# Sparse attention over listed keys: half steps taken in pairs, and a new order of the steps' parts on the PE

## The chip, the cores and the metric

The kernel runs on one core of a Trainium2 chip. The time is the device time of one execution, in microseconds. Before the change the median of three runs is 2332.32 us (2330.68 to 2333.52). The engines are named as in the profile: PE multiplies matrices (PEld is its weight loads, which run beside the multiplications), ACT is ScalarE, DVE is VectorE, POOL is GpSimd, which issues the gathers here, and SP issues the plain transfers.

## The reference

One layer of graph attention with 8 heads over 4096 nodes, in which a node attends only to its neighbours, and then a mixture of 8 experts of which each node takes two. All is f32. The change concerns the attention:

```python
q = jnp.einsum('nd,hdk->hnk', node_matrix, Wqs)        # 8 heads of 64
k = jnp.einsum('nd,hdk->hnk', node_matrix, Wks)
v = jnp.einsum('nd,hdk->hnk', node_matrix, Wvs)
scores = jnp.einsum('hqk,hmk->hqm', q, k) * kd ** (-0.5)
scores = scores + IDENTITY_BIAS * eye - MASK_VAL * (1.0 - adj)
att = jax.nn.softmax(scores, axis=-1)
return jnp.einsum('hqm,hmk,hko->qo', att, v, Wo)
```

The adjacency is sparse, and a node's own entry always counts as set.

## The kernel before

The kernel has three stages. The first normalizes x, computes q, k and v, writes a row of k and v per node to memory, and makes a list of keys for each tile of 128 queries: the nodes that any query of the tile has as a neighbour, 128 of them to a "key tile". The second is the attention over those lists, with the end of each tile of queries (division by the sums, product with Wo, routing to experts) mixed into its steps. The third is the experts. Only the second changes.

A list has three parts: keys that only the first 64 queries of the tile need, keys that both halves need, and keys that only the last 64 need. A step takes one key tile `(i, c)`. For keys of both halves it works on 128 queries (a full step), for the others on 64 (a half step, `half_of` gives the half). `c = -1` is the step of the tile's own 128 nodes, the diagonal, a full one. The list lengths give 32 diagonal, 134 full and 229 half steps, 395 in all.

For each step POOL gathers the 128 rows of k and v (4 KB each) and, unless they were packed before, those of the mask. PE then transposes k, multiplies it with q, ACT takes the exponential, DVE multiplies by the mask, PE multiplies with the values into the tile's output `po`, and DVE adds the weights to the sums `acc`. q lies in a tile of twice its size: for each pair of heads p, `q_in[:, p, 0]` holds the even head's 64 rows with zeros below, `q_in[:, p, 1]` the odd head's with zeros above. (Two memory clears on POOL write the zeros once.)

```python
        def turn(n):
            kT[n] = work.tile([P, NP, P], F32, tag="kT", bufs=3, name=f"kT_{n}")
            pk = ps_k.tile([P, 2, TB], F32, tag="k", name=f"pk_{n}")
            for p in range(NP):
                for r in range(2):
                    half = slice(r * KD, (r + 1) * KD)
                    nc.tensor.transpose(
                        pk[:, r, ts(p, KD)], kv[n][half, ts(p, P)], ident[half, half]
                    )
            nc.scalar.copy(
                kT[n].rearrange("k p (r j) -> k r p j", r=2),
                pk[:, :, : NP * KD].rearrange("k r (p j) -> k r p j", p=NP),
            )

# ... (queries(i, c): the 128 or 64 columns of the step)
        def scores(n):
            i, c = items[n]
            full = half_of(i, c) is None
            q = queries(i, c)
            k = kT.pop(n)
            if c < 0:
                e = two.tile([P, H, P], F32, tag="acc", name=f"acc_{i}")
                acc[i] = e
            else:
                e = work.tile([P, H, P], F32, tag="e", name=f"e_{i}_{c}")
                if not full:
                    e = e.rearrange("p h q -> p (h q)")[:, : H * QH]
                    e = e.rearrange("p (h q) -> p h q", h=H)
            es[n] = e
            if full:
                s = [
                    ps_s.tile([P, NP, P], F32, tag="s", name=f"s{r}_{i}_{c}") for r in range(2)
                ]
                for p in range(NP):
                    for r in range(2):
                        rows = slice(r * KD, (r + 1) * KD)
                        nc.tensor.matmul(
                            s[r][:, p, :], k[rows, p, :], q_in[i][rows, p, r, :],
                            start=True, stop=True,
                        )
                for r in range(2):
                    nc.scalar.activation(
                        e.rearrange("p (a r) q -> p r a q", r=2)[:, r], s[r], AF.Exp
                    )
            else:
                s = ps_s.tile([P, NP, 2, QH], F32, tag="s", name=f"s_{i}_{c}")
                for p in range(NP):
                    nc.tensor.matmul(
                        s[:, p], k[:, p, :], q_in[i][:, p, :, q], start=True, stop=True
                    )
                nc.scalar.activation(e, s.rearrange("p a r q -> p (a r) q"), AF.Exp)
        def masked(n):
            i, c = items[n]
            e, m = es[n], mask.pop(n)
            if c < 0:
                nc.vector.tensor_max(m, m, eye_d)
            m = mask_part(m, i, c)
            nc.vector.tensor_mul(e, e, m.unsqueeze(1).to_broadcast(e.shape))
        def values(n):
            i, c = items[n]
            e = es.pop(n)
            if c < 0:
                po[i] = ps_o.tile([P, NP, P], F32, tag="o", name=f"po_{i}")
            v = kv.pop(n)[:, H * KD :]
            q = queries(i, c)
            for h in range(H):
                p, r = divmod(h, 2)
                nc.tensor.matmul(
                    po[i][r * KD : (r + 1) * KD, p, q], v[:, ts(h, KD)], e[:, h, :],
                    start=(c < 0 and p == 0), stop=(c == listed[i] - 1),
                    skip_group_check=True,
                )
            if c >= 0:
                nc.vector.tensor_add(acc[i][:, :, q], acc[i][:, :, q], e)

```

The loop works three steps ahead with the transposes and two with the scores; `fetch` starts the gathers nine steps ahead. `later` issues the parts of finished tiles, of which those after 1, 3 and 5 steps multiply on PE, and the jobs of the routing, one in a step without such a part.

```python
        def later(n):
            busy = False
            for n0, i in left:
                piece(i, n - n0)
                busy = busy or n - n0 in (1, 3, 5)
            if jobs and not busy:
                then = jobs.pop(0)()
                if then:
                    first_of_step.append(then)
        for n in range(3):
            turn(n)
        for n in range(2):
            scores(n)
            masked(n)
        loads = [(e, c) for e in range(E) for c in range(DC)]
        for n, (i, c) in enumerate(items):
            begin()
            if n + AHEAD < len(items):
                fetch(n + AHEAD)
            if c == 2 and i + 1 < NT:
                load_q(i + 1)
            if c == min(7, listed[i] - 1):
                load_x(i)
            if n >= 56 and n % 7 == 0 and loads:
                e, d = loads.pop(0)
                nc.sync.dma_start(out=w1[:, e, d], in_=W1[e, ts(d, P), :])
            if c < 0 and i:
                osb[i - 1] = single.tile([P, NP, P], F32, tag="o", name=f"o_{i - 1}")
                nc.scalar.copy(osb[i - 1], po.pop(i - 1))
            if n + 3 < len(items):
                turn(n + 3)
            if n + 2 < len(items):
                scores(n + 2)
            values(n)
            later(n)
            if n + 2 < len(items):
                masked(n + 2)
            if c == listed[i] - 1:
                left.append((n, i))
        osb[NT - 1] = single.tile([P, NP, P], F32, tag="o", name=f"o_{NT - 1}")
        nc.scalar.copy(osb[NT - 1], po.pop(NT - 1))

```

The pools of PSUM: three buffers for scores (`ps_s`), one for the transposes (`ps_k`, two banks), one for the output `po`, two for the ends of tiles.

## Time and profile before

The profile covers one execution, whose span is 2307.7 us.

| engine | busy us | share of the span |
|---|---|---|
| PE | 2102.1 | 91% |
| PEld | 1389.0 | 60% |
| DVE | 1266.7 | 55% |
| POOL | 1030.9 | 45% |
| ACT | 933.3 | 40% |

The attention loop takes from about 465 to 1692 us of it, the experts from about 1800 us to the end. The groups of instructions that matter here, from the fifth part of the page (all in that loop):

| what | count | busy us | mean ns |
|---|---|---|---|
| PE transposes of k (L917) | 2904 | 177.5 | 239 |
| PE scores of half steps, K = 128 (L964) | 1832 | 276.2 | 295 |
| PE scores of full steps, K = 64 (L952) | 2144 | 160.2 | 283 |
| PE products with the values (L987) | 5808 | 322.4 | 250 |
| ACT copy of the transposed k (L920) | 395 | 232.3 | 588 |
| ACT exponentials of full (L957) and half (L967) steps | 268 and 229 | 146.9 and 137.9 | 597 and 602 |
| DVE product with the mask (L975) | 363 | 322.3 | 888 |
| DVE sum of the weights (L993) | 363 | 320.5 | 883 |

How to read it: an f32 product is recorded as two matmuls and two weight loads. PE's matmuls are pipelined and their ends are modelled, so a busy PE is not PE at its peak; what can be read closely is when an instruction starts. "64*128 64x128" is a stationary operand of 64 rows and 128 columns, and a moving one of 64 rows and 128 columns. Diagonal steps have names of their own in the profile, and are not in all of these counts.

### The profile page before, as it was taken

How to read it: one execution, taken by the hardware profiler on the slowest of the kernel's cores; microseconds unless marked ns; L12 is line 12 of the kernel's file. 1: busy time of each engine (PE TensorE's matmuls, PEld its weight loads, DVE VectorE, ACT ScalarE, POOL GpSimd, SP SyncE). 2: the span in 40 equal slices, each digit the busy share in tenths (PEclk: the TensorE clock that was granted, in tenths of full speed). 3: DMA queues.
4: the chain of work that ended last, by engine and by line, in shares of the span. 5: the costliest groups of instructions: out<-in, count | busy, mean ns of one | idle time of the engine just before them, and what ended most of it. 6: DMA issues, size and time to landing. Idle time of an engine off the chain costs nothing. (4 is left out here: it accounts for less than half of the span.)

```text
span 2307.7 us, 48617 instructions
## 1 busy us (share of the span) xinstructions
PE 2102.1 (91%) x18796; PEld 1389.0 (60%) x18796; DVE 1266.7 (55%) x2297; ACT 933.3 (40%) x1709; POOL 1030.9 (45%) x1080
## 2 busy tenths in 40 slices
PE   7988897899999889999999999998957999999998
PEld 3434443387777777777777777776733444444444
DVE  4686676166666656656656666665652332323332
ACT  2644443355445445445445454544421222222221
POOL 1044434667666566565555655566521121212112
PEclk9998999899999999999899999999978999999999
DMA  7777877667777777778777877767666656665564
GB/s 293 313 264 269 273 261 248 207 192 212 225 242 233 221 235 234 220 219 234 211 234 223 237 220 225 224 197 225 186 237 148 134 137 136 137 138 134 137 132 91
DMA packets 214383, 481.13 MB, mean 208 GB/s; under 512 B 49234, under 2 KB 81234, under 8 KB 210052
## 3 DMA queue, kind: packets, MB, share of 16 engines
q0 software_dynamic: 79232, 242.18, 37.1%
q1 hardware_dynamic: 133764, 233.68, 33.0%
q8 instruction: 153, 2.51, 0.4%
q10 hardware_dynamic: 1152, 2.10, 0.3%
q14 instruction: 82, 0.67, 0.1%
HBM read 400.43 MB, written 77.42 MB: 207 GB/s over the span
## 5 line engine op out<-in xcount | busy, mean ns | idle before, releaser
L228 POOL DMA_INDIRECT kv<-kv_d,key_of x363 | 405.8, 1118 | 384.4 <-PE po L987 220.5
L975 DVE TENSOR_TENSOR e<-e,mask 128x512 f32<-128x512 f32 (+1 forms) x363 | 322.3, 888 | 308.1 <-ACT e L967 144.3
L920 ACT COPY kT<-pk 128x512 f32<-128x512 f32 x395 | 232.3, 588 | 370.6 <-PE pk L917 216.6
L987 PE MATMUL po<-e,kv 128*64 128x64 f32 (+1 forms) x5808 | 322.4, 250 | 18.2 <-issue 17.9
L1387 POOL DMA_INDIRECT out_dram<-y,r x71 | 110.6, 1558 | 473.7 <-ACT y L1386 453.2
L993 DVE TENSOR_TENSOR acc<-acc,e 128x512 f32<-128x512 f32 (+1 forms) x363 | 320.5, 883 | 2.5 <-PE sums L1012 0.9
L228 POOL DMA_INDIRECT mask<-in_adjT_dram,mask_of x234 | 282.3, 1206 | 72.9 <-issue 63.4
L987 PEld LDWEIGHTS po<-e,kv 128*64 128x64 f32 x5808 | 251.9, 139 | 70.1 <-issue 25.8
L964 PE MATMUL s<-q,kT 128*128 128x128 f32 x1832 | 276.2, 295 | 3.1 <-issue 2.7
L1351 PE MATMUL ph<-w,xT 128*128 x568 | 257.9, 597 | 0.7 <-ACT xT L207 0.7
L1380 PE MATMUL py<-w,hT 128*128 x568 | 255.6, 593 | 0.9 <-DVE hT L1365 0.9
L964 PEld LDWEIGHTS s<-q,kT 128*128 128x128 f32 x1832 | 230.8, 197 | 19.4 <-issue 3.5
L917 PE MATMUL pk<-ident,kv 64*128 64x64 f32 x2904 | 177.5, 239 | 49.0 <-ACT kT L920 30.1
L917 PEld LDWEIGHTS pk<-ident,kv 64*128 64x128 f32 x2904 | 123.9, 141 | 120.2 <-issue 72.0
L228 POOL DMA_INDIRECT pm<-in_adjT_dram,mask_of x129 | 126.2, 978 | 149.6 <-DMA packed_h<-pm 80.0
L957 ACT ACTIVATE e<-s 128x512 f32<-128x512 f32 x268 | 146.9, 597 | 72.1 <-PE s L952 30.1
L1385 DVE TENSOR_TENSOR y<-py,bb 128x512 f32<-128x512 f32 x71 | 49.1, 692 | 225.6 <-PE py L1380 225.6
L967 ACT ACTIVATE e<-s 128x512 f32<-128x512 f32 x229 | 137.9, 602 | 79.4 <-PE s L964 43.9
L359 DVE TENSOR_REDUCE flags<-adjT 128x64 f32<-128x4096 f32 x32 | 141.0, 4408 | 52.3 <-DMA adjT<-in_adjT_dram 52.3
L1351 PEld LDWEIGHTS ph<-w,xT 128*128 128x128 f32 x568 | 103.1, 192 | 103.8 <-issue 102.7
L1380 PEld LDWEIGHTS py<-w,hT 128*128 128x128 f32 x568 | 102.5, 190 | 104.0 <-issue 102.8
L952 PE MATMUL s<-q,kT 64*128 64x128 f32 x2144 | 160.2, 283 | 4.6 <-issue 2.6
(598 smaller groups left out, 2614.8 us busy)
## 6 DMA issues: line engine op xcount, KB each, us to landing
adjT<-in_adjT_dram SPq DMA_DIRECT2D x32, 2048.0 KB
bb<-in_L_ffn_b_dram SPq DMA_DIRECT2D x142, 256.0 KB
r<-xs_d SPq DMA_DIRECT2D x71, 258.0 KB
kv_d<-kv SPq DMA_DIRECT2D x32, 512.0 KB
xt<-in_x_dram SPq DMA_DIRECT2D x32, 256.0 KB
qT_d<-qT SPq DMA_DIRECT2D x8, 1024.0 KB
q<-qT_d SPq DMA_DIRECT2D x64, 128.0 KB
xr<-in_x_dram SPq DMA_DIRECT2D x32, 256.0 KB
```

Source lines behind the costliest of these rows:

```text
L228: nc.gpsimd.indirect_dma_start(out=to, out_offset=None, in_=src, in_offset=bass.IndirectOffsetOnAxis(ap=of[:, at[i] + c : at[i] + c + 1], ...
L359: nc.vector.tensor_reduce(flags[g][:, :, j, :], adj_in.pop(i).rearrange("p c (h q) -> p h c q", h=2), axis=AX.X, op=ALU.max,)
L917: nc.tensor.transpose(pk[:, r, ts(p, KD)], kv[n][half, ts(p, P)], ident[half, half])
L920: nc.scalar.copy(kT[n].rearrange("k p (r j) -> k r p j", r=2), pk[:, :, : NP * KD].rearrange("k r (p j) -> k r p j", p=NP),)
L952: nc.tensor.matmul(s[r][:, p, :], k[rows, p, :], q_in[i][rows, p, r, :], start=True, stop=True,)
L957: nc.scalar.activation(e.rearrange("p (a r) q -> p r a q", r=2)[:, r], s[r], AF.Exp)
L964: nc.tensor.matmul(s[:, p], k[:, p, :], q_in[i][:, p, :, q], start=True, stop=True)
L975: nc.vector.tensor_mul(e, e, m.unsqueeze(1).to_broadcast(e.shape))
L987: nc.tensor.matmul(po[i][r * KD : (r + 1) * KD, p, q], v[:, ts(h, KD)], e[:, h, :], start=(c < 0 and p == 0), stop=(c == listed[i] - 1), s ...
L993: nc.vector.tensor_add(acc[i][:, :, q], acc[i][:, :, q], e)
L1351: nc.tensor.matmul(ph, xTs[b][:, c, :], w1[:, bass.ds(es[b], 1), c, :], start=(c == 0), stop=(c == DC - 1),)
L1380: nc.tensor.matmul(py, hTs[b][:, c, :], w2[:, bass.ds(es[b], 1), c, :], start=(c == 0), stop=(c == HC - 1),)
```

## The change

Half steps are worked on by two. A unit is a diagonal, a full key tile, or a pair of half ones (one alone where their number is odd); pairs and full ones alternate evenly over a tile's list. A pair has one exponential per parity of heads, one product with the mask per parity, one copy of the transposed keys, and one place in the loop. All scores are now taken from 64 rows of q and k, even heads in the upper and odd ones in the lower rows, so that q needs no zeros and comes in one transfer. The two parities lie in two banks, and each has its own exponential and its own product with the mask, the second of which is issued a step later. In a step PE is given the transposes of the unit after next, the values of this one, the ends of tiles and the scores of the unit after next. The copy of the output follows the tile's last values at once. Gathers run eleven key tiles ahead. A step with a pair may take a job of the routing beside another piece.

It is for giving PE fewer and larger steps, with fewer changes between kinds of work, and the same work of ACT and DVE in larger operations for pairs.

The diff, cut to its core:

```diff
-    AHEAD = 9
-    items = [(i, c) for i in range(NT) for c in range(-1, listed[i])]
+    KEPT = 11
+
+    units = []
+    for i in range(NT):
+        units.append((i, [-1]))
+        alone = [c for c in range(listed[i]) if half_of(i, c) is not None]
+        pairs = [alone[j : j + 2] for j in range(0, len(alone), 2)]
+        both = [[c] for c in range(listed[i]) if half_of(i, c) is None]
+        few, total = len(pairs), len(pairs) + len(both)
+        for j in range(total):
+            if j * few // total < (j + 1) * few // total:
+                units.append((i, pairs.pop(0)))
+            else:
+                units.append((i, both.pop(0)))
+    keys_of = [(n, j) for n, (i, cs) in enumerate(units) for j in range(len(cs))]
+    first_key = [sum(len(cs) for _, cs in units[:n]) for n in range(len(units))]
+    fetched = []
... (load_q in one transfer; fetch by keys, the masks of a pair in one tile; pools)
         def turn(n):
+            i, cs = units[n]
+            kT[n] = work.tile([P, 2, NP, P], F32, tag="kT", bufs=2, name=f"kT_{n}")
             pk = ps_k.tile([P, 2, TB], F32, tag="k", name=f"pk_{n}")
+            for j in range(len(cs)):
+                for p in range(NP):
+                    for r in range(2):
+                        half = slice(r * KD, (r + 1) * KD)
+                        nc.tensor.transpose(
+                            pk[:, r, ts(j * NP + p, KD)], kv[n, j][half, ts(p, P)],
+                            ident[half, half],
+                        )
+            m = len(cs) * NP
             nc.scalar.copy(
+                kT[n].rearrange("k j p (r c) -> k r (j p) c", r=2)[:, :, :m],
+                pk.rearrange("k r (m c) -> k r m c", c=KD)[:, :, :m],
             )
         def queries(i, c):
             h = half_of(i, c)
             return slice(0, P) if h is None else ts(h, QH)
+        def width(n):
+            i, cs = units[n]
+            return P if half_of(i, cs[0]) is None else len(cs) * QH
+        def heads(e):
+            return e.rearrange("p (a r) q -> p r a q", r=2)
         def scores(n):
+            i, cs = units[n]
+            w = width(n)
             k = kT.pop(n)
+            ss[n] = []
+            for r in range(2):
+                s = ps_s.tile([P, NP * P], F32, tag="s", name=f"s{r}_{n}")
+                ss[n].append(s[:, : NP * w].rearrange("p (a q) -> p a q", a=NP))
+            for j, c in enumerate(cs):
+                m = w // len(cs)
                 for p in range(NP):
                     for r in range(2):
                         rows = slice(r * KD, (r + 1) * KD)
                         nc.tensor.matmul(
+                            ss[n][r][:, p, ts(j, m)], k[rows, j, p, :],
+                            q_in[i][rows, p, queries(i, c)], start=True, stop=True,
                         )
+            if cs[0] < 0:
+                es[n] = acc[i] = two.tile([P, H, P], F32, tag="acc", name=f"acc_{i}")
+                nc.vector.tensor_max(mask[n], mask[n], eye_d)
+            else:
+                e = work.tile([P, H * P], F32, tag="e", name=f"e_{n}")
+                es[n] = e[:, : H * w].rearrange("p (h q) -> p h q", h=H)
+        def masked(n, r):
+            w = width(n)
+            e = heads(es[n])[:, r]
+            nc.scalar.activation(e, ss[n][r], AF.Exp)
+            nc.vector.tensor_mul(
+                e, e, mask[n][:, :w].unsqueeze(1).to_broadcast([P, NP, w])
+            )
+        def values(n):
+            i, cs = units[n]
+            e = es.pop(n)
+            last = n + 1 == len(units) or units[n + 1][0] > i
+            if cs[0] < 0:
+                po[i] = ps_o.tile([P, NP, P], F32, tag="o", name=f"po_{i}")
+            m = width(n) // len(cs)
+            for j, c in enumerate(cs):
+                v = kv.pop((n, j))[:, H * KD :]
+                for h in range(H):
+                    p, r = divmod(h, 2)
+                    nc.tensor.matmul(
+                        po[i][r * KD : (r + 1) * KD, p, queries(i, c)], v[:, ts(h, KD)],
+                        e[:, h, ts(j, m)], start=(c < 0 and p == 0),
+                        stop=(last and j == len(cs) - 1), skip_group_check=True,
                     )
+            if last:
+                osb[i] = single.tile([P, NP, P], F32, tag="o", name=f"o_{i}")
+                nc.scalar.copy(osb[i], po.pop(i))
+                left.append((n, i))
+            for j, c in enumerate(cs):
+                if c >= 0:
+                    a = acc[i][:, :, queries(i, c)]
+                    nc.vector.tensor_add(a, a, e[:, :, ts(j, m)])
... (in this part the removed lines are left out: they are the code shown above)
-            if jobs and not busy:
+            if jobs and (not busy or n < len(units) and len(units[n][1]) > 1):
                 then = jobs.pop(0)()
                 if then:
                     first_of_step.append(then)
 
-        for n in range(3):
+        for n in range(2):
             turn(n)
-        for n in range(2):
             scores(n)
-            masked(n)
+            masked(n, 0)
+            if n == 0:
+                masked(n, 1)
         loads = [(e, c) for e in range(E) for c in range(DC)]
-        for n, (i, c) in enumerate(items):
+        for n, (i, cs) in enumerate(units):
             begin()
-            if n + AHEAD < len(items):
-                fetch(n + AHEAD)
-            if c == 2 and i + 1 < NT:
+            fetch(first_key[n] + KEPT)
+            if n and cs[0] >= 0 and units[n - 1][1][0] < 0 and i + 1 < NT:
                 load_q(i + 1)
-            if c == min(7, listed[i] - 1):
+            if n + 1 == len(units) or units[n + 1][0] > i:
                 load_x(i)
-            if n >= 56 and n % 7 == 0 and loads:
-                e, d = loads.pop(0)
-                nc.sync.dma_start(out=w1[:, e, d], in_=W1[e, ts(d, P), :])
-            if c < 0 and i:
-                osb[i - 1] = single.tile([P, NP, P], F32, tag="o", name=f"o_{i - 1}")
-                nc.scalar.copy(osb[i - 1], po.pop(i - 1))
-            if n + 3 < len(items):
-                turn(n + 3)
-            if n + 2 < len(items):
-                scores(n + 2)
+            for k in range(first_key[n], first_key[n] + len(cs)):
+                if k >= 56 and k % 7 == 0 and loads:
+                    e, d = loads.pop(0)
+                    nc.sync.dma_start(out=w1[:, e, d], in_=W1[e, ts(d, P), :])
+
+            if n + 2 < len(units):
+                turn(n + 2)
+            if n + 1 < len(units):
+                masked(n + 1, 1)
             values(n)
             later(n)
-            if n + 2 < len(items):
-                masked(n + 2)
-            if c == listed[i] - 1:
-                left.append((n, i))
-        osb[NT - 1] = single.tile([P, NP, P], F32, tag="o", name=f"o_{NT - 1}")
-        nc.scalar.copy(osb[NT - 1], po.pop(NT - 1))
+            if n + 2 < len(units):
+                scores(n + 2)
+                masked(n + 2, 0)
```

## The prediction

> **What bounds the kernel now.** I read the engine shares first, then the stretch in which the changed code runs, then the PE's own instructions in order of time, and the waits last. The chain of work that ended last holds only the final transfer on this page, so it says nothing about the middle of the run.
>
> The attention loop (line L987, the products with the values, marks its first and last step) runs from 465 to 1692 us. The busy times of that stretch, engine by engine:
>
> ```profile
> core 0: us, PE busy (x) PEld busy (x) DVE busy (x) ACT busy (x) POOL busy (x), PEclk, DMA share, GB/s
> 465.00:1692.00 1227.00, 1138.58 (x15341) 916.94 (x15339) 796.80 (x1241) 604.63 (x1201) 741.05 (x639) 0.97 0.74 220
> ```
>
> PE is busy for 1139 of 1227 us. Nothing else passes 800. The stage is PE's, so I need the PE's cost of one step. Two cuts of the time line of weight loads give it: first two full steps (all 128 queries), then two half steps (64 queries). Columns: start, length, operation, how many.
>
> ```profile
> 719.11 0.33 PEld L917 LDWEIGHTS pk<-ident,kv 64*128 64x128 f32 x8 [0.76 <-issue]
> 719.36 0.98 PEld L952 LDWEIGHTS s<-q,kT 64*128 64x128 f32 x16
> 720.46 0.85 PEld L987 LDWEIGHTS po<-e,kv 128*64 128x64 f32 x16
> 721.48 0.33 PEld L917 LDWEIGHTS pk<-ident,kv 64*128 64x128 f32 x8 [0.17 <-issue]
> ```
>
> ```profile
> 738.36 0.30 PEld L721 LDWEIGHTS pl<-gather,l 128*128 128x128 f32 x2
> 738.67 0.32 PEld L917 LDWEIGHTS pk<-ident,kv 64*128 64x128 f32 x8
> 739.07 0.97 PEld L964 LDWEIGHTS s<-q,kT 128*128 128x128 f32 x8
> 740.15 0.55 PEld L987 LDWEIGHTS po<-e,kv 128*64 128x64 f32 x16
> 740.77 0.42 PEld L702 LDWEIGHTS pt_b<-ident,rows 128*128 128x128 f32 x4
> ```
>
> Reading start to start, a full step is transposes 0.25 + scores 1.10 + values 1.02 = 2.37 us. A half step is 0.40 + 1.08 + 0.62 = 2.10 us: it has half the queries and costs nearly as much. Two things show. Scores cost 1.1 us either way: the half step multiplies zeros (its K is 128 with half of q zeroed). And between blocks of different tile shape there are 0.15 to 0.20 us in which nothing starts: 8 transposes take 0.24 us, but the next block comes after 0.40 where the scores use all 128 rows, after 0.25 where they use 64 rows like the transposes.
>
> The mean lengths of weight loads, by shape, over the same stretch:
>
> ```profile
> L987 PEld LDWEIGHTS po<-e,kv 128*64 128x64 f32 x5792 | 251.3, 139 | 69.9 <-issue 25.8 <-DVE acc L975 0.7 <-DVE acc L993 0.7
> L964 PEld LDWEIGHTS s<-q,kT 128*128 128x128 f32 x1822 | 228.8, 196 | 19.1 <-issue 3.3
> L952 PEld LDWEIGHTS s<-q,kT 64*128 64x128 f32 x2144 | 140.1, 192 | 7.1 <-issue 3.3 <-ACT e L957 3.3
> L917 PEld LDWEIGHTS pk<-ident,kv 64*128 64x128 f32 x2880 | 122.4, 140 | 110.4 <-issue 71.8 <-ACT kT L920 27.0 <-ACT e L957 0.9
> L721 PEld LDWEIGHTS pl<-gather,l 128*128 128x128 f32 x58 | 8.6, 188 | 3.1 <-issue 1.7 <-ACT e L967 0.2
> ```
>
> A score's weights (128 columns of f32, 64 or 128 rows) take about 53 ns longer to load than those of a transpose or of the values. L721 isolates it: two loads in 0.30 us, of 188 each, so the second starts about 0.11 us after the first, though the matmul between them moves only 8 columns. So **a score load occupies its tile for about 0.107 us** whatever it multiplies. This decides the sum below.
>
> Last, what PE itself waits for:
>
> ```profile
> PE pk L917 <- ACT kT L920: 22.1, 24, 3.2
> PE po L987 <- ACT o L1150: 15.5, 18, 3.5
> ...
> PEld pk L917 <- ACT kT L920: 28.8, 39, 3.4
> PEld po L987 <- issue: 27.1, 63, 1.2
> PEld po L987 <- ACT o L1150: 19.4, 19, 3.7
> ```
>
> PE and PEld tell of the same waits, so the copy of a tile's output (L1150) costs some 18 us, the copies of kT some 25.
>
> **What the Trainium skill says.** "TensorEngine Tiling (Array Packing)", Key Properties: changing the tiling mode drains the TensorE, while tiles of one mode load and multiply in parallel. The trace agrees: the 0.15 to 0.20 us at each change of shape, none between transposes and 64-row scores. "TensorE: Matmul & The Clock Gate", section LDWEIGHTS: a load costs its columns, P/1.2 ns, not its rows, so 107 ns for 128 columns. L721 agrees, and 64-row and 128-row loads have the same mean (192 and 196); the transposes' loads of 128 columns are shorter (140), which that formula doesn't give.
>
> **The change, part by part.** From the lists: 229 half keys become 102 pairs and 25 singles; with 134 full keys and 32 diagonals that is 293 units in place of 395 steps.
>
> 1. Scores of half keys: 8 matmuls of K = 64 and 64 queries instead of 4 of K = 128 and 128 columns, each two passes. Sixteen passes lie in two row tiles, eight in each, at a load of 0.107. L952 shows the pitch: its 16 loads are over after 0.98, the last of them takes 0.19, so (0.98 - 0.19)/7 = 0.113 for each pair, eight pairs 0.90 us. The eight loads of L964 have the same pitch, (0.97 - 0.19)/7 = 0.111, 0.89 us. The moving side is halved, but the loads set the pitch: no gain here.
> 2. Changes of shape. The new order is transposes, values, scores, and the next transposes have the scores' shape. A unit has two changes instead of three in a half step. Pair: transposes 2 x 0.25 = 0.51, change 0.15, values 2 x 0.48 = 0.96, change 0.15, scores 1.79; sum 3.56 us against 2 x 2.095 = 4.19. 102 pairs save 64 us. Single: 0.24 + 0.15 + 0.47 + 0.15 + 0.90 = 1.91 against 2.10, 25 save 5. Full: 0.24 + 0.15 + 0.82 + 0.20 + 0.90 = 2.31 against 2.36 to 2.37; with the diagonals 166 x 0.05 = 8. **PE: -77 us.**
> 3. The output copy now follows the last values at once, with a block of scores and one of transposes (over 1.1 us) before the next tile's values want its bank; the copy takes 0.59. **-18 us.**
> 4. New: scores(n+2) stand in the same step as transposes(n+2), with only values between; now the copy has a whole step. Counted from the start of the transposes: exp of the unit before starts at 0.25 (0.31 after its last score in the half steps here, less the change that is gone) and takes 0.60; then the kT copy, 0.59, or for a pair 0.163 + 1024 x 0.83 ns = 1.01 (an estimate, from 269 ns at 128 and 588 at 512 elements); then 0.05 to 0.1 to PE. Scores can start at 1.55, with a pair at 1.97. PE is there at 1.41 (both full), 1.77 (both pairs) or 1.68 (full values, transposes of a pair): 0.14 to 0.29 of waiting, unless an end of a tile (0.32 to 3.6 us) fills it. Each tile has six such pieces, 186 in all, so some 107 units are bare: 107 x 0.2 = 21. Where ACT also copies x2T (0.59) or normalizes (0.81) first, 30 times each, the end of 0.36 or 0.59 us covers only part: 30 x 0.43 + 30 x 0.40 = 25. **+46 us.**
> 5. DVE: masks become 586 in place of 395; by 1224 ns at 1024 and 691 at 512 elements a further operation costs 158 ns: +30 us, to 827 of a stage of about 1178. Beside PE. ACT: 102 copies fewer by their fixed 0.163, 25 exponentials more: -13, beside PE too.
> 6. POOL and transfers: the same gathers, one more buffer of keys. Two memory clears fall away and q comes in one transfer; that is before or beside the loop: 0.
>
> Sum: -77 - 18 + 46 = **-49 us**, so 2332 - 49 = **2283 us**.
>
> **Rivals.** (a) The loads are hidden after all, and half scores run at the transposes' pitch (16 in 0.48): 229 x 0.42 = 96 us more, 2283 - 96, **about 2187**. For it: the operand shape is the transposes'. Against it: the 188 ns of L721. (b) ACT becomes the bound within each step, because kT's copy sits behind an exp in the same step: 0.35 us on all 293 units is 103 us, 2332 - 95 + 103 = **about 2340**. For it: ACT stood still for DVE up to 4.7 us when the routing's small exponential came; now PE has less slack behind it. Against it: ACT is busy for half of the stage. (c) POOL or the transfers: 741 us busy and about 0.30 us between two gathers, 639 x 0.30 = 192, makes 933, and the queues' 0.74 would be 0.77. A pair takes POOL 2 x 1.42 + 1.3 x 1.51 = 4.8 us, more than PE's 3.56; the keys fetched ahead and full units and ends even that out. If they didn't for half of the pairs, 51 x 1.2 = 61 us would come back: 2283 + 61, **about 2344**. (d) DVE has 2.6 us for a full unit against PE's 2.37; two in a row lose 0.2 us; 30 such would be 6 us, **about 2289**.
>
> **Range and chances.** The savings rest on gaps read directly; the +46 rests on an interplay I can only lay out, and could be 0 (2237) or 95 (2332). Both ends make the range, 2235 to 2332; it leaves (a) outside, and nearly all of (b) and (c). The limit of 2% is 2286, right at my value, so faster by over 2% gets 0.50, within 2% 0.46; slower by over 2% (above 2379) needs (b) and (c) together, 0.04.
>
> **What will show it.** The scores of half keys as 3664 matmuls of 64x64, starting in twos every 0.11 us: step 1 (0.06 would be rival a). No idle time between scores and transposes, two gaps a unit: step 2. The wait of values for the output copy gone: step 3. A new wait of the scores for the kT copy, near 46 us in total; over 100 would be rival b. POOL's waits for PE shrinking to nothing while transposes wait for gathers would be (c). The loop should take about 1178 us. A loop over 1227 makes the prediction wrong in sign; under 1120 it has missed a whole term.

## The result, and the profile after

The kernel after takes 2475.18 us (2464.39 to 2476.05) beside 2331.5 us for the kernel before: a ratio of 1.061, 95% interval 1.058 to 1.064. The change was predicted to save 49 us and costs 144.

The loss lies in the attention loop alone. Its busy times in the profile after (columns as in the prediction: start and end, length, busy time of each engine with its instructions, mean granted clock, share of the DMA engines, GB/s):

```profile
467.00:1855.00 1388.00, 1158.87 (x17175) 964.18 (x17175) 826.43 (x1416) 576.38 (x1125) 692.70 (x634) 0.90 0.63 193
```

The loop grew from 1227 to 1388 us, by 161. Two things are to be seen. PE's idle time (length less PE busy) was 1227 - 1139 = 88 us and is 1388 - 1159 = 229: **+141 us of waiting**. PE's busy time grew by 20 us, although it has less to do, and the clock fell from 0.97 to 0.90. In the loop 264 us run at half clock, before the change 65; PE was busy for 239 and 56 us of these. Work at half clock takes twice its time, so the clock costs PE about (239 - 56)/2: **+92 us of clock**, an estimate. With it the prediction's own saving can be read off: 20 - 92 = -72 us, near its -77 for fewer changes of shape.

The saving is visible in PE's weight loads, in a stretch with a full clock (start, length, operation, how many):

```profile
1005.66 0.63 PEld L927 LDWEIGHTS pk<-ident,kv 64*128 64x128 f32 x16
1006.36 0.85 PEld L995 LDWEIGHTS po<-acc,kv_-1_9559 128*64 128x64 f32 x16
...
1008.11 1.86 PEld L963 LDWEIGHTS s<-q,kT 64*128 64x128 f32 x32 [0.35 <-ACT kT L932]
1009.83 0.39 PEld L927 LDWEIGHTS pk<-ident,kv 64*128 64x128 f32 x8
1010.28 0.92 PEld L995 LDWEIGHTS po<-e,kv 128*64 128x64 f32 x16
```

The scores of a pair take 1.72 us from their start to the transposes' (1.79 predicted), with no gap at that border; and a pair's 16 transposes with the change after them 0.70 (0.66 predicted). All half keys' scores are there, by form (count, busy time, mean ns, then idle time before them and what ended it):

```profile
L963 PE MATMUL s<-q,kT 64*128 64x64 f32 x3664 | 245.2, 285 | 58.7 <-ACT kT L932 50.5 <-issue 7.3
L963 PE MATMUL s<-q,kT 64*128 64x128 f32 x2624 | 226.5, 321 | 62.4 <-ACT kT L932 54.1 <-issue 6.5 <-ACT e L978 0.5
```

But the scores begin with a wait for ACT's copy of kT. The waits of that profile (engine, operation and line, what ended the wait; us in total, times, longest):

```profile
POOL kv L240 <- PE po L995: 471.0, 196, 8.8
...
PEld s L963 <- ACT kT L932: 136.9, 142, 4.6
PE s L963 <- ACT kT L932: 105.9, 93, 4.4
ACT test L1035 <- DVE rinv L1033: 80.0, 29, 2.8
ACT e L978 <- PE po L995: 74.9, 20, 7.8
ACT e L978 <- remote: 74.7, 16, 8.6
...
PEld pt_b L712 <- ACT rows L200: 28.8, 14, 4.9
...
ACT kT L932 <- remote: 28.2, 20, 3.9
```

The scores wait 137 us for kT in weight loads (106 in matmuls), where 46 were predicted. The wait for the output copy is gone. The wait of the ends of tiles for ACT's normalized row has grown (`pt_b`, 28.8 us; 5.4 before), and ACT's copy of the sums waits for DVE's reciprocal of the same PSUM tile (80 us). POOL waits for PE, so no transfer sets the pace.

**What one wait does.** The same profile, PE alone, and then the windows of its clock:

```profile
947.98 1.11 PE L963 MATMUL s<-q,kT 64*128 64x64 f32 x16 [2.17 <-ACT kT L932]
948.92 0.42 PE L927 MATMUL pk<-ident,kv_-1_9043 64*128 64x64 f32 x8
949.27 1.98 PE L995 MATMUL po<-e,kv 128*64 128x64 f32 x32
951.18 1.85 PE L963 MATMUL s<-q,kT 64*128 64x128 f32 x16
```

```profile
945.84:949.25 3.41, 1.27 (x24) 1.22 (x24) 1.48 (x3) 1.70 (x4) 1.12 (x2) 1.00 0.96 331
949.25:952.67 3.42, 3.42 (x50) 3.28 (x48) 3.21 (x6) 1.05 (x3) 1.69 (x2) 0.50 0.78 234
952.67:956.08 3.41, 1.51 (x34) 1.30 (x34) 0.69 (x1) 1.52 (x3) 1.97 (x3) 1.00 0.88 268
```

PE waits 2.17 us. In the next window of 3.41 us its clock is 0.50, and the 16 scores at 951.18, usually 0.9 us, take 1.7. So part of this wait is paid for again in the next window. The Trainium skill, "TensorE: Matmul & The Clock Gate", Part 1: The HAM clock gate, says that the clock is granted in full or at half, by a free-running window of 3413 ns, from how busy PE has been. The trace agrees on both: every change of clock lies on that grid, and only 1.0 and 0.5 occur. The page puts the cold state after at least one idle window; here a window in which PE was busy for 1.27 us is enough.

**What ACT did ahead of that wait**, in the same stretch, and PE's weight loads beside it:

```profile
940.88 0.60 ACT L978 ACTIVATE e<-s 128x512 f32<-128x512 f32 x1
946.86 0.60 ACT L978 ACTIVATE e<-s 128x512 f32<-128x512 f32 x1 [5.38 <-PE po L995]
947.35 0.58 ACT L932 COPY kT<-pk 128x512 f32<-128x512 f32 x1
```

```profile
941.03 1.86 PEld L963 LDWEIGHTS s<-q,kT 64*128 64x128 f32 x32 [0.70 <-ACT kT L932]
942.76 0.39 PEld L927 LDWEIGHTS pk<-ident,kv 64*128 64x128 f32 x8
943.21 0.20 PEld L995 LDWEIGHTS po<-e,kv 128*64 128x64 f32 x4
943.86 0.19 PEld L995 LDWEIGHTS po<-e,kv 128*64 128x64 f32 x3 [0.45 <-issue]
944.62 0.30 PEld L995 LDWEIGHTS po<-e,kv 128*64 128x64 f32 x5 [0.56 <-issue]
```

The pair's scores had their last weights at 942.9 us, yet the exponential starts at 946.86 and the copy behind it comes late. The named releaser, the values of another unit, ends at 945.8 and gives the exponential no operand. I counted all copies of kT and exponentials that start over 0.5 us after both ACT's operation before and the last product that PE had begun into a tile of their kind: 131 in the loop, 200 us in total; in the kernel before 130 and 178 us. (There the next scores have often begun by then; counted from each operation's own operand it is 155 and 207 us.)

**In these late starts ACT waits for a signal of PE.** The trace also holds the times at which PE signals, by a semaphore, that a product for another engine is done. The last such signal before that exponential comes at 946.83 us, 0.03 us ahead of it, and the one before that at 940.88, although three products that signal lie in between with recorded ends of 943.03, 943.28 and 945.82. It is so in 130 of the 131: a signal of PE lies at most 0.12 us ahead of ACT's start, where only 11% of all moments in the loop have one so near. In `b_order`, a run below without late starts, PE's signals come 0.01 to 0.05 us after the recorded ends, at most 0.27. Whether the products themselves end late is not shown, as PE's ends are modelled; its values from 943.21 on falter too, for no recorded cause. Transfers of instructions don't account for it: one ends in 22 of the 131 gaps, and by chance it would be 21. **ACT loses as much by these late signals before the change.** But there its copy had a whole step to spare.

### The profile page after: what moved, and what is told of

The parts are those of the page before. It is cut to its first block, busy times and chain, and to the rows that moved or that the text cites. A ratio compares the mean times of both kernels' runs of the same rounds, so it can differ in the third digit from the quotient of the medians.

```text
span 2472.9 us, 51990 instructions
## 1 busy us (share of the span) xinstructions
PE 2126.4 (86%) x20628; PEld 1437.7 (58%) x20628; DVE 1299.8 (53%) x2488; ACT 904.8 (37%) x1632; POOL 984.3 (40%) x1076
## 5 line engine op out<-in xcount | busy, mean ns | idle before, releaser
L979 DVE TENSOR_TENSOR e<-e,mask 128x512 f32<-128x512 f32 (+1 forms) x522 | 345.5, 666 | 503.4 <-ACT e L978 434.5
L240 POOL DMA_INDIRECT kv<-kv_d,key_of x363 | 375.6, 1035 | 563.1 <-PE po L995 471.0
L963 PE MATMUL s<-q,kT 64*128 64x64 f32 (+1 forms) x6320 | 475.8, 301 | 132.8 <-ACT kT L932 105.9
L963 PEld LDWEIGHTS s<-q,kT 64*128 64x128 f32 x6320 | 421.9, 207 | 200.0 <-ACT kT L932 136.9
L978 ACT ACTIVATE e<-s 128x512 f32<-128x512 f32 (+1 forms) x522 | 305.0, 584 | 553.6 <-PE s L963 237.7
L995 PE MATMUL po<-e,kv 128*64 128x64 f32 (+1 forms) x5808 | 341.0, 261 | 32.8 <-issue 30.5
L932 ACT COPY kT<-pk 128x512 f32<-128x512 f32 (+1 forms) x293 | 215.1, 734 | 74.0 <-remote 28.2
L927 PE MATMUL pk<-ident,kv 64*128 64x64 f32 x2904 | 148.6, 237 | 2.3 <-issue 1.8
L1396 ACT ACTIVATE y<-y,gate 128x512 f32<-128x512 f32 x71 | 51.2, 721 | 213.1 <-DVE y L1395 213.1
L207 ACT COPY xT<-pt_e 128x512 f32<-128x512 f32 x71 | 41.5, 585 | 230.9 <-PE pt_e L206 228.0
```

Source lines behind the costliest of these rows:

```text
L240: nc.gpsimd.indirect_dma_start(out=to, out_offset=None, in_=src, in_offset=bass.IndirectOffsetOnAxis(ap=of[:, at[i] + c : at[i] + c + 1], ...
L927: nc.tensor.transpose(pk[:, r, ts(j * NP + p, KD)], kv[n, j][half, ts(p, P)], ident[half, half],)
L932: nc.scalar.copy(kT[n].rearrange("k j p (r c) -> k r (j p) c", r=2)[:, :, :m], pk.rearrange("k r (m c) -> k r m c", c=KD)[:, :, :m],)
L963: nc.tensor.matmul(ss[n][r][:, p, ts(j, m)], k[rows, j, p, :], q_in[i][rows, p, queries(i, c)], start=True, stop=True,)
L978: nc.scalar.activation(e, ss[n][r], AF.Exp)
L979: nc.vector.tensor_mul(e, e, mask[n][:, :w].unsqueeze(1).to_broadcast([P, NP, w]))
```

## Experiments

The runs were made in five groups; each ratio is to the kernel before in the same group, which took 2332, 2182, 2312, 2314 and 2337 us. In the second group ACT had not one of those late starts, in any of its four kernels, though the fifth group ran on the same chip and had them; the kernel after was not run in the second. Times are therefore compared by ratio, and mechanisms within a group where possible. "Half clock" is the time at 0.50 within the loop, "late" the sum of ACT's late starts as counted above.

| run | group | ratio (95%) | loop us | half clock us | late us |
|---|---|---|---|---|---|
| after, the run predicted | - | 1.061 (1.058-1.064) | 1388 | 264 | 200 |
| after_2 | 3 | 1.055 (1.050-1.060) | 1356 | 237 | 170 |
| after_3 | 4 | 1.049 (1.045-1.054) | 1364 | 267 | 178 |
| a_test | 1 | 1.054 (1.051-1.058) | 1383 | 275 | 218 |
| a_ahead | 1 | 1.047 (1.041-1.052) | 1358 | 208 | 185 |
| a_both | 1 | 1.041 (1.037-1.046) | 1331 | 178 | 205 |
| a_fill | 2 | 1.020 (1.017-1.023) | 1140 | 65 | 0 |
| a_old | 3 | 1.055 (1.051-1.060) | 1345 | 287 | 192 |
| a_oldfill | 3 | 1.050 (1.046-1.054) | 1343 | 246 | 204 |
| a_pairs | 4 | 1.021 (1.017-1.025) | 1276 | 215 | 201 |
| a_pairsfill | 5 | 1.020 (1.017-1.023) | 1294 | 212 | 220 |
| b_order | 2 | 1.091 (1.088-1.093) | 1295 | 93 | 0 |
| b_order_2 | 4 | 1.067 (1.061-1.072) | 1379 | 143 | 57 |
| b_rows | 1 | 1.020 (1.015-1.024) | 1294 | 271 | 165 |
| b_rows_2 | 3 | 1.020 (1.015-1.024) | 1277 | 247 | 153 |
| b_rows128 | 2 | 0.988 (0.986-0.990) | 1072 | 21 | 0 |
| b_rows128_2 | 4 | 1.008 (1.005-1.011) | 1254 | 97 | 186 |
| b_ocopy | 5 | 0.996 (0.995-0.998) | 1240 | 75 | 193 |
| b_best | 2 | 0.985 (0.983-0.987) | 1066 | 10 | 0 |

Two theories stood at the start. W: the waits for ACT are the loss. C: the clock is, and it falls because half keys' scores now move 64 columns where they moved 128.

### The waits in the kernel after

`a_test` gives ACT its copy of the sums before DVE its reciprocal:

```diff
-                nc.vector.reciprocal(rinv[i], sums[i])
                 test = single.tile([P, P], F32, tag="test", name=f"test_{i}")
-                nc.scalar.activation(test, sums.pop(i), AF.Copy, accum_out=fine[:, i, 0:1])
+                nc.scalar.activation(test, sums[i], AF.Copy, accum_out=fine[:, i, 0:1])
+                nc.vector.reciprocal(rinv[i], sums.pop(i))
```

> The changed kernel with one pair of lines swapped: ACT's check of the sums (test from sums) is issued before DVE's reciprocal of the same PSUM tile, so that DVE waits for ACT and not ACT for DVE. Theory W (PE loses because scores wait in their own step for ACT's copy of kT, ACT is held up, and the clock then falls for want of work): the 80 us for which ACT stood before that check go, some 40 to 90 us come off, 2385 to 2435 us, and the time at half clock in the loop falls from 264 to about 200 us. Theory C (the clock falls because half keys' scores of 64 columns fill less of the array, waits or not): hardly any gain, 2450 to 2475 us, half clock as before.

ACT's wait of 80 us is gone, the wait for kT is still 127 us, and the ratio of 1.054 lies among those of the kernel after itself (1.049 to 1.061). That wait was beside the path.

`a_ahead` makes the transposes a unit earlier, so that the scores need no copy of their own step, and `a_both` joins it with `a_test`:

```diff
+        turn(0)
         for n in range(2):
-            turn(n)
+            turn(n + 1)
             scores(n)
...
-            if n + 2 < len(units):
-                turn(n + 2)
+            if n + 3 < len(units):
+                turn(n + 3)
```

> The changed kernel with the transposes one unit further ahead (unit n+3 in step n, two copies of kT as before), so that the scores of a step use a copy made in the step before; everything else as changed. Theory W: the waits of the scores for kT's copy (137 us of weight loads) nearly vanish, the half clock falls to about 100 us, and the kernel comes to 2270 to 2340 us. Theory C: the waits vanish, but the half clock stays above 200 us and the kernel above 2370 us.

> Both: transposes one unit further ahead, and ACT's check before DVE's reciprocal. Theory W: the savings of 77 us in PE's blocks show at last, 2230 to 2300 us, half clock under 100 us. Theory C: 2350 us or more, half clock above 200 us.

The wait for kT is gone in both, but only 1.4 and 1.9 points of the 6.1 with it (against the later runs of the kernel after, less). In `a_ahead` PE stands idle at other borders instead: from the values to the row's transposes 45 us, from the values to another piece 36, within the scores 21. C's forecast holds for `a_ahead`; in `a_both` the half clock, 178 us, is below what C forecast. W, as put, falls: what is waited for at one place is waited for at the next, while the order leaves the ends of tiles no slack either.

`after_2` and `after_3` are the kernel after, unchanged, beside later experiments:

> The changed kernel again, as the measure for the three beside it: as a ratio to the kernel before 1.05 to 1.09 under every theory; b_order, the order alone, had 1.09, and the theory of the waits (W) says that the pairs give part of it back.

> The changed kernel, as the measure for the three beside it. 1.05 to 1.07 times the kernel before as in its two earlier measurements, unless the engines' stops without a recorded cause are missing here as in the calls with b_order; then theory W says 1.03 to 1.07 all the same, as its waits come from the order.

### The order alone

`b_order` and, in another group, `b_order_2` are the kernel before with nothing but the new order:

```diff
-        for n in range(3):
-            turn(n)
         for n in range(2):
+            turn(n)
             scores(n)
...
-            if n + 3 < len(items):
-                turn(n + 3)
             if n + 2 < len(items):
-                scores(n + 2)
+                turn(n + 2)
             values(n)
             later(n)
             if n + 2 < len(items):
+                scores(n + 2)
                 masked(n + 2)
```

> The kernel before with the new order alone: in a step transposes of the step after next, values, ends, scores of the step after next; no pairs, scores of half steps as before over 128 rows. Theory W (waits for kT's copy in the step of its use): waits of the scores for that copy near 100 us, the clock a little lower through them, 2400 to 2450 us. If only the filling counts (theory C alone): 2325 to 2345 us, half clock under 100 us.

> The kernel before with the new order alone, beside the changed kernel in one call. Theory W (the order is what costs): 1.06 to 1.10, above the changed kernel. If pairs or half rows cost most of it: at most 1.03.

It costs more than the whole change: 1.091 and 1.067, the latter beside `after_3` with 1.049. Waits of `b_order_2`, and its loop:

```profile
PEld s L964 <- ACT kT L920: 76.2, 114, 3.4
...
PEld s L952 <- ACT kT L920: 64.6, 87, 3.5
PE s L964 <- ACT kT L920: 56.1, 85, 3.3
...
PE s L952 <- ACT kT L920: 46.8, 75, 3.3
...
PE pt_b L702 <- ACT rows L200: 31.2, 17, 4.5
PE po L987 <- ACT o L1149: 30.1, 27, 3.6
```

```profile
467.00:1846.00 1379.00, 1143.82 (x15369) 930.99 (x15371) 796.04 (x1237) 589.19 (x1204) 711.78 (x639) 0.95 0.65 196
```

PE idles 1379 - 1144 = 235 us, +147 beside the kernel before, the same as in the kernel after (+141). PE's new waits explain it: kT 56 + 47 = 103, rows 31 - 4 = 27, output 30 - 15.5 = 14.5. And `b_order` shows it without any late start of ACT. Of its 262 starts of scores that come within 0.15 us of the end of their copy, 251 had ACT idle for at most 0.3 us since the last transpose, and wait 65 us, 0.26 each: ACT is simply the slower one within the step. (The other 11 wait 18 us behind an operation of ACT that itself waited for DVE.) Counted alike, the kernel after has 168 such starts. At 56 of them ACT was at work, and they wait 5 us, 0.10 each; 29 wait 24 us behind an operation that waited for DVE; at 83, which wait 92 us, ACT had stood idle for another reason, by the count above PE's late signal. So pairs do give ACT the time that the prediction laid out for them; what breaks through is mostly the late signals, for which the new order leaves no slack.

### Halves of rows and the moving columns

`b_rows` is the kernel before with the half keys' scores taken from 64 rows and 64 columns; `b_rows_2` repeats it:

```diff
-                s = ps_s.tile([P, NP, 2, QH], F32, tag="s", name=f"s_{i}_{c}")
+                s = [
+                    ps_s.tile([P, NP, QH], F32, tag="s", name=f"s{r}_{i}_{c}") for r in range(2)
+                ]
                 for p in range(NP):
-                    nc.tensor.matmul(
-                        s[:, p], k[:, p, :], q_in[i][:, p, :, q], start=True, stop=True
-                    )
-                nc.scalar.activation(e, s.rearrange("p a r q -> p (a r) q"), AF.Exp)
+                    for r in range(2):
+                        rows = slice(r * KD, (r + 1) * KD)
+                        nc.tensor.matmul(
+                            s[r][:, p, :], k[rows, p, :], q_in[i][rows, p, r, q],
+                            start=True, stop=True,
+                        )
+                for r in range(2):
+                    nc.scalar.activation(
+                        e.rearrange("p (a r) q -> p r a q", r=2)[:, r], s[r], AF.Exp
+                    )
```

> The kernel before with one part of the change alone: the scores of half steps as eight products of 64 rows and 64 queries into two banks, with two exponentials of 256 elements each, no pairs, the old order. Theory W: PE saves the change of shape between transposes and scores, 229 x 0.15 = 34 us, against 35 us more of ACT beside it: 2290 to 2325 us, half clock under 100 us. Theory C: the clock falls here too, over 150 us at half clock, and the kernel is slower than before, 2350 us or more.

> The kernel before with half steps' scores in halves of the rows and 64 moving columns, again, on the chip of these runs. Theory C: slower than before or equal, ratio 1.00 to 1.03, half clock above 120 us in the loop, where the same kernel with 128 moving columns had a ratio of 0.988 and 20 us. If filling does not matter: 0.98 to 0.99.

`b_rows128` and `b_rows128_2` move all 128 columns for those keys and read half of the product, so 64 columns are wasted:

```diff
-                    ps_s.tile([P, NP, QH], F32, tag="s", name=f"s{r}_{i}_{c}") for r in range(2)
+                    ps_s.tile([P, NP, P], F32, tag="s", name=f"s{r}_{i}_{c}") for r in range(2)
...
-                            s[r][:, p, :], k[rows, p, :], q_in[i][rows, p, r, q],
+                            s[r][:, p, :], k[rows, p, :], q_in[i][rows, p, r, :],
...
-                        e.rearrange("p (a r) q -> p r a q", r=2)[:, r], s[r], AF.Exp
+                        e.rearrange("p (a r) q -> p r a q", r=2)[:, r], s[r][:, :, q], AF.Exp
```

> As the kernel before with half steps' scores in halves of the rows, but every such product moves all 128 queries (64 of them for nothing) and the exponentials read their 64: same weight loads, same waits, same ACT and DVE work, twice the moving columns. Theory C (the clock follows how full the moving columns keep the array): the time at half clock falls from 271 to under 100 us, and 2382 becomes 2290 to 2320 us, below the kernel before, as the change of shape between transposes and scores is saved. If the clock falls for another reason (the row halves as such, or waits): about 2380 us, half clock near 270 us.

> The kernel before with half steps' scores in halves of the rows and 128 moving columns, to stand beside the two runs of 64 moving columns (1.0195 and 1.0197 times the kernel before, 247 and 271 us at half clock). Theory C: 0.97 to 1.00 and under 100 us at half clock also where the engines stop without a recorded cause. If the earlier gain came from the absence of those stops: 1.01 to 1.02 and about 250 us.

The loops of `b_rows` and `b_rows128_2`:

```profile
468.00:1763.00 1295.00, 1210.63 (x17163) 999.40 (x17163) 799.06 (x1240) 624.15 (x1429) 730.99 (x639) 0.90 0.68 209
```

```profile
466.00:1720.00 1254.00, 1162.96 (x17154) 940.01 (x17155) 796.88 (x1243) 625.13 (x1429) 726.96 (x639) 0.96 0.72 216
```

The idle time is alike, 84 and 91 us, nearly that of the kernel before. The busy time falls by 48 us; of it 258 us lie at half clock in `b_rows` and 86 in `b_rows128_2`, so the clock takes some 129 and 43. More moving work makes it faster: the loads take the time anyway, and the columns moved beside them keep the clock up. That is C. The saved change of shape shows too: from the start of a block of transposes to the next block, the weight loads take 111 us in all in `b_rows128_2` and 146 before (medians 0.24 and 0.39 us). That `b_rows128_2` still loses 0.8% goes with stops of PE within the scores, 29 us against 6, mostly without a recorded releaser; in the second group, without them, the same kernel gains 1.2%.

### Pairs, in the old order

`a_fill` is `a_both` with the second key of a pair moved twice (its columns also fill the first's place, which is then overwritten); `a_old` is the kernel after, with `a_test`'s edit and the prologue of `a_ahead`, in the order of before (transposes, scores, values, ends); and `a_oldfill` joins that with the filling:

```diff
-            for j, c in enumerate(cs):
+            for j, c in reversed(list(enumerate(cs))):
...
+                        if j:
+                            q2 = q_in[i][rows, p, queries(i, c)].unsqueeze(1)
+                            nc.tensor.matmul(
+                                ss[n][r][:, p, :].rearrange("p (a q) -> p a q", a=2),
+                                k[rows, j, p, :], q2.to_broadcast([KD, 2, QH]),
+                                start=True, stop=True,
+                            )
+                            continue
```

```diff
-            if n + 2 < len(units):
-                turn(n + 2)
+            if n + 3 < len(units):
+                turn(n + 3)
             if n + 1 < len(units):
                 masked(n + 1, 1)
+            if n + 2 < len(units):
+                scores(n + 2)
             values(n)
             later(n)
             if n + 2 < len(units):
-                scores(n + 2)
                 masked(n + 2, 0)
```

> As the changed kernel with transposes one unit further ahead and ACT's check first (2428 us), but in a pair the second key's scores are taken first with their 64 queries moved twice, 128 columns, and the first key's then written over one half: same loads, three quarters instead of half of the columns filled. Theory C: half clock from 178 to under 110 us, 30 to 50 us less, 2375 to 2400 us. Otherwise: unchanged within 10 us.

> Pairs and scores in halves of the rows as changed, but PE in the old order: transposes of unit n+3, scores of unit n+2, values of unit n, ends of tiles; ACT's check before DVE's reciprocal. The number of changes of shape is the same as in the new order, as transposes and scores have one shape. Theory W (the new order makes PE wait for ACT and DVE: kT's copy, normalized rows, reciprocals): the waits of scores for kT and of the ends for ACT go, the ratio to the kernel before falls to 0.96 to 1.01, the loop's half clock stays above 100 us if theory C also holds. If the pairs themselves are what costs: above 1.03.

> As the pairs in the old order, and the second key of a pair is multiplied first with its 64 queries moved twice (128 columns). Same loads, same waits. Theory C (a less filled array lowers the clock): half clock at least 50 us less than with pairs in the old order alone and the ratio lower by 0.01 to 0.03. If the filling does not matter: same within 0.005.

`a_fill` keeps 1.020 even in the group where ACT was never late, with a clock of 0.97: its ends of tiles wait 35 us for the normalized rows. `a_old` misses what was expected by far. The wait for kT has gone, and another stands in its place:

```profile
PEld s L963 <- ACT e L978: 45.7, 74, 3.7
PE s L963 <- ACT e L978: 32.6, 42, 3.6
```

Two banks for each unit of three in all, one of them held until an exponential of the next step: the scores wait for a bank. `a_pairs` issues both exponentials in the step of the scores, as the kernel before does, and `a_pairsfill` adds the filling:

```diff
-            if n + 1 < len(units):
-                masked(n + 1, 1)
...
                 masked(n + 2, 0)
+                masked(n + 2, 1)
```

> Pairs and scores in halves of the rows in the old order (transposes n+3, scores n+2, values n, ends), with both exponentials and both masks of a unit at the end of the step that makes its scores, as before the change; ACT's check first. If the split of the exponentials over two steps made scores wait for their banks (46 us in the pairs of the old order): those waits go and the ratio falls from 1.055 by 0.02 to 0.04, to 1.01 to 1.035. If the half clock of pairs with 64 moving columns is what keeps them slow (theory C): still 1.03 to 1.055, with over 200 us at half clock. On a call without the stops: 0.97 to 1.01.

> The kernel a_pairs (pairs and halves of rows in the old order, exponentials of a step together) with the second key of each pair moved twice, so that its loads have 128 moving columns again. Theory of the clock: time at half clock in the loop falls from 215 to under 150 us and the ratio from 1.021 to 1.00 to 1.01. Rival, scores that wait for banks and exponentials (31 to 46 us), which the edit leaves: ratio 1.02 as before.

That gives back 3.4 points (1.055 to 1.021, in different groups). The filling then gives nothing: 212 us at half clock beside 215, 1.020 beside 1.021, and in `a_oldfill` half a point, within the intervals. So in pairs C does not explain the clock that remains low. The weight loads of the pairs' scores still wait 31 us for exponentials there (22 and 11 us in `a_pairsfill`), and PE stands idle for 40 us within its scores in both, part of it in these waits; what holds the clock down stays open.

### The early output copy, and a faster version

```diff
-            if c < 0 and i:
-                osb[i - 1] = single.tile([P, NP, P], F32, tag="o", name=f"o_{i - 1}")
-                nc.scalar.copy(osb[i - 1], po.pop(i - 1))
...
             values(n)
+            if c == listed[i] - 1:
+                osb[i] = single.tile([P, NP, P], F32, tag="o", name=f"o_{i}")
+                nc.scalar.copy(osb[i], po.pop(i))
```

`b_ocopy` is the kernel before with this edit, `b_best` is `b_rows128` with it.

> The kernel before with one edit: ACT gets the copy of a tile's output right after the tile's last values. Step 3 of the prediction (the wait of the next values for that copy was worth about 18 us): ratio 0.990 to 0.995, and the wait of PE for the output copy (15.5 us, 19.4 us in weight loads) gone. If other waits take its place: ratio 0.998 to 1.002.

> As b_rows128, and the copy of a tile's output is given to ACT right after the tile's last values instead of at the next step's start. Theory C: some 15 us less than b_rows128 by the 18 us that values waited for that copy, 2270 to 2305 us. If ACT's queue makes other things late instead: no gain over b_rows128.

```profile
PEld po L987 <- ACT o L1155: 11.3, 14, 1.6
PE po L987 <- ACT o L1155: 8.4, 13, 1.4
```

In `b_ocopy` about half of the wait is left and half of the 18 us gained, 0.4% or 9 us, less than was expected; the wait (15.5 and 19.4 us before) is gone in the order of the change, where a block of scores stands between. `b_ocopy` is faster than both kernels of this study. `b_best` is so by 1.5%, measured in the second group only; `b_rows128_2` suggests that it would not hold everywhere.

## Why the prediction was wrong

1. **Half keys' scores are bound by their loads: right.** 3664 matmuls of 64x64 in the loop, pairs in 1.72 us. Rival (a) is out. What the step didn't see is that the halved columns, free in time, cost clock.
2. **Fewer changes of shape, -77: right in size, wrongly credited to the order.** About -72 by the balance above, and -63 when each kind of block of the loop is counted at the 5th percentile of its length at full clock (1069 us before, 1006 after). Scores of 64 rows share the transposes' shape in the old order as well, where `b_rows128_2` shows the saving.
3. **The output copy, -18: right inside the new order** (the wait is gone), half of it in the old one.
4. **"+46" is the step that failed.** It let the exponential start 0.31 us after its last score and the copies follow at ACT's usual pace, which made 0.14 to 0.29 us of waiting at some 107 bare units. Where ACT was at work, that held: 0.10 us each. But the hand-over from PE to ACT is not always so short: at 131 places ACT started up to 3.9 us late, at a late signal of PE. The first profile already had waits of ACT's copies of up to 4.5 and 5.2 us:

```profile
ACT kT L920 <- PE pk L917: 213.7, 145, 4.5
...
ACT kT L920 <- remote: 42.8, 15, 5.2
```

PE's wait for kT was only 22 us there because a whole step lay between. The prediction took that 22 as the size of the hazard; it was what the slack let through. With the slack gone PE waits 106 us for kT and more at the ends, +141 in all. And where no signal is late the new order alone still costs: 9.1% in `b_order`, with ACT the slower one within the step.

5. and 6. **DVE 827 predicted, 826 measured, beside PE; POOL and transfers no bound: right.** Rivals (c) and (d) are out.

And **a term is missing**: the clock, +92 us. The prediction took PE's durations at full clock throughout, though the profile gave 0.97. The half clock grows with the new order's waits alone (143 us in `b_order_2`) and more with the 64-column scores alone (271 us in `b_rows`). Rival (b) was right that scores would wait for ACT, but that its 103 us lie so close to the 106 measured is luck: it put 0.35 us on every unit, and the waits are few and long. Its total of 2340 lacked the clock and the ends. The sum with these terms: -72 + 141 + 92 = +161 us in the loop (the -72 being what the other two leave).

Not settled: what delays PE's signals (131 late starts of ACT in one run, none in another group with like programs), what the whole change costs without such delays, and what holds the clock low in `a_pairs`.

## What to carry to other kernels

A short wait behind a long slack measures the slack and not the hazard: before an order is tightened, look at how late the producer itself starts at its worst, and price the wait at that. When PE sets the time, a new wait can also cost clock in the windows after it: 147 us of new waiting came with 78 us more at half clock in `b_order_2`. And where loads set the pitch, moving fewer columns gains no time and can lose clock.

## What the runs showed of the hardware

- A lean window is followed by one at half clock. For each 3.41 us window at full clock I summed the columns of its matmuls (transposes left out), each weighted by the share of the array's rows and columns it uses, taken at 0.43 us for 512 columns (the pace of the products with Wo here), as a part of the window. Below 0.2 all were followed by half clock (7 of 7 before, 25 of 25 after); from 0.25 to 0.3 2 of 3 and 12 of 19; above 0.4 none (of 299 and 232). The mean was 0.61 before and 0.49 after. This is a correlation; only `b_rows` against `b_rows128` changed the columns alone and moved the clock, and `a_pairsfill` did not.
- Two readers of one PSUM tile, ACT's copy and DVE's reciprocal, ran one after the other in the order of issue: 80 us of waiting for ACT, gone when turned round, and worth nothing here.
- A like program ran with no late start of ACT in one group (`b_order`) and with 65 in another (`b_order_2`, 57 us). The kernel before differed between those groups by 133 us. In every run with late starts the trace lacks 12 to 23% of ACT's signals, in the four without them 0.4 to 1.4%; whether the tracing has a part in the delays, no run here tests.
